# Graph attention with edge features on one core: how the eight heads' scores of each edge are made leaky and summed

## The chip, the cores and the metric

The kernel runs on one core of a Trainium2 chip. The metric is the device time of one execution in microseconds (us), taken as the median of several runs. The profile that is read here is one further execution under the hardware profiler. The engines are TensorE (PE for its products, PEld for its weight loads, which overlap them), VectorE (DVE), ScalarE (ACT), GpSimd (POOL) and SyncE (SP, which issues most DMAs).

## The reference

One graph attention layer over 12,500 nodes and 412,500 edges (each node has an edge to itself), with 128 features a node, 64 an edge, and 8 heads. The attention weight of an edge comes from a small network with two leaky rectifiers; the softmax runs over all edges of the graph at once.

```python
h = node_features @ Wn + bn
q = node_features @ Wq + bq
k = node_features @ Wk + bk
v = node_features @ Wv + bv
eh = edge_features @ We + be
src, tgt = (edge_index[0], edge_index[1])
attn_in = jnp.concatenate([q[src], k[tgt], eh], axis=-1)
hmid = jax.nn.leaky_relu(attn_in @ A1 + b1, SLOPE)
scores = jax.nn.leaky_relu(hmid @ A2 + b2, SLOPE)
w = jax.nn.softmax(scores.mean(axis=-1), axis=0)
out = jax.ops.segment_sum(w[:, None] * v[tgt], src, num_segments=num_nodes)
y = h + out
...
return gamma * (y - mu) / jnp.sqrt(var + EPS) + beta
```

The change touches the line of `scores` and the mean over the heads behind it.

## The kernel before

Edges arrive sorted by their target. The kernel cuts them into four chunks (`CHUNKS`). A first stage goes through a chunk's edges in tiles of 128: TensorE makes for every edge a row of 257 numbers (the place of its source in a block, 128 hidden values, 128 values of `v`), ScalarE copies it out of PSUM (line 652), and GpSimd scatters 128 rows at a time into a table in HBM (line 603), ordered by blocks of source nodes.

A second stage then works through the table. There are 98 blocks of source nodes, and each chunk has its part of every block, so 392 blocks in all (`blocks`), numbered through the chunks. A block of chunk 0, 1, 2 or 3 holds `ct` = 8, 11, 11 or 7 tiles of 128 edges, and its tiles are taken in `nq` = 2, 3, 3 or 2 groups of four (`QUAD`).

The second stage of chunk c runs beside the first stage of chunk c + 1; that of chunk 3 runs alone at the end. `interleave` mixes the jobs step by step when the program is built, and the engines' queues keep the order in which it was written (`manual_schedule`). Inside the second stage a plan by hand sets the order: `at(when, turn_, job, i)` puts a job of block i into a step, and jobs of one step are ordered by `turn_`. [...]

The steps of a block that matter here, in their order:

- `turn` (line 719, TensorE): four transposes (723) and three products (726) put the hidden values of four tiles into `h_ps`.
- `steep` (729): ScalarE makes `low`, 0.2 times these (734), VectorE takes the maximum and writes it back into `rows_of` (735).
- `heads_of` (738, TensorE, 743): product with `A2`. The result `s_ps` is one PSUM bank of 128 x 512; group q of four tiles has rows 32q to 32q + 31, of which the first 8 are the heads, and the columns are 4 x 128 edges.
- `add_bias` (747, ScalarE, 750): adds `b2` and copies `s_ps` to `z` in SBUF.
- `leaky` (752, VectorE, 754): z = max(0.2 z, z) over 32nq x 512.
- `by_slot` (756, TensorE, 760): for each of the four columns of tiles a product of `z` with `heads`, a matrix of zeros and ones, which sums the eight heads and turns edges onto partitions. Each fp32 product of this kind has two records of a weight load and two of a product in the profile, eight pairs a block.
- `scores` (764, VectorE, 768 to 774): a mask for empty slots, the older maximum, the sum of the two, and the largest of each partition, `top`.
- `turn_top` (777, TensorE), `top_of_all` (781, VectorE), `spread_top` (784, TensorE), `exponentials` (790 and 793 on VectorE, 795 on ScalarE): the largest score of the whole block, and the exponentials.
- `weights` (809, VectorE) and `products` (818, TensorE): the weighted sum of the values for an older block; `add_sums` (823, VectorE) adds it to `acc`.

In the steps of the next block, `steep` of its first group stands just ahead of `by_slot` in the plan, and on VectorE line 735 of that group stands just ahead of `scores`. Behind `scores` VectorE has line 823 or `weights`, then line 781. The turn of the next group follows `turn_top` on TensorE.

Of the kernel before, what the change touches and what calls it, by code (L numbers as in the profile page):

```python
# [13 lines left out]
ALU = mybir.AluOpType  # L14
AX = mybir.AxisListType
# [4 lines left out]
P = 128  # L20
D = 128
DE = 64
H = 8
EPS = 1e-5
SLOPE = 0.2
# [5 lines left out]
QUAD = 4  # L31
# [67 lines left out]
def kernel(ctx: ExitStack, tc: tile.TileContext, n_edges, x, src, dst, ea, w_nv, w_qt, w_kt,  # L99
# [12 lines left out]
    nc = tc.nc  # L112
# [10 lines left out]
    for i, share in enumerate(CHUNKS):  # L123
        n = NG - g0 if i == len(CHUNKS) - 1 else max(1, round(NG * share))
# [7 lines left out]
    blocks = []  # L132
# [40 lines left out]
    ident = const.tile([P, P], FP, name="ident")  # L173
# [3 lines left out]
    ones = const.tile([P, P], FP, name="ones")  # L177
# [47 lines left out]
    heads = const.tile([P, 4], FP, name="heads")  # L225
# [336 lines left out]
    most_of = late.tile([P, NTN], FP, name="most_of")  # L562
# [116 lines left out]
    def second_stage():  # L679


        rows_of, qws, plss, state = {}, {}, {}, {}
# [66 lines left out]
            state["z"] = p3.tile([P, 512], FP, name="z")  # L749
            nc.scalar.activation(state["z"][:n, :], state["s_ps"][:n, :], AF.Identity, bias=b2_col[:n, :])  # L750

        def leaky(i):
            z = state["z"][:32 * blocks[i][3], :]
            nc.vector.scalar_tensor_tensor(z, z, SLOPE, z, op0=ALU.mult, op1=ALU.max)  # L754

        def by_slot(i):

            nq = blocks[i][3]
            for j in range(QUAD):
                nc.tensor.matmul(state["s_ps"][:, 0:nq * QUAD].rearrange("p (q j) -> p j q", j=QUAD)[:, j, :],  # L760
                                 lhsT=state["z"][:32 * nq, ts(j, P)], rhs=heads[:32 * nq, 0:nq], start=True, stop=True,
                                 skip_group_check=True)

        def scores(i):

            _, b, ct, _, _ = blocks[i]
            none = ps.tile([P, most_tiles], FP, name="none")[:, 0:ct]
            nc.vector.tensor_scalar(none, rows_of[i][:, 0:ct, 0:1].rearrange("p j r -> p (j r)"), 0.0, -1e30,
                                    op0=ALU.is_equal, op1=ALU.mult)
            state["score", i] = score = ps.tile([P, most_tiles + 1], FP, name="score")  # L770
            nc.vector.tensor_copy(score[:, ct:ct + 1], most_of[:, b:b + 1])
            nc.vector.tensor_add(score[:, 0:ct], state["s_ps"][:, 0:ct], none)
            state["top"] = ps.tile([P, 1], FP, name="top_of")
            nc.vector.tensor_reduce(state["top"], score[:, 0:ct], AX.X, ALU.max)

        def turn_top(i):
            nc.tensor.transpose(state["s_ps"][0:1, P:2 * P], state["top"], ident)

        def top_of_all(i):
            state["top1"] = ps.tile([1, 1], FP, name="top1_of")  # L780
            nc.vector.tensor_reduce(state["top1"], state["s_ps"][0:1, P:2 * P], AX.X, ALU.max)

        def spread_top(i):
            nc.tensor.matmul(state["s_ps"][:, 2 * P:2 * P + 1], lhsT=ones[0:1, :], rhs=state["top1"], start=True, stop=True,
                             skip_group_check=True)

        def exponentials(i):
            _, b, ct, _, _ = blocks[i]
            before = (b - 1) % NTN
            nc.vector.tensor_max(most_of[:, b:b + 1], state["s_ps"][:, 2 * P:2 * P + 1], most_of[:, before:before + 1])  # L790

            shift = ps.tile([P, 1], FP, name="shift_of")
            nc.vector.tensor_scalar(shift, most_of[:, b:b + 1], -1.0 / H, None, op0=ALU.mult)
            score = state["score", i][:, 0:ct + 1]
            nc.scalar.activation(score, score, AF.Exp, bias=shift, scale=1.0 / H)
# [32 lines left out]
        def at(when, turn_, job, *args):  # L828
            plan_of.setdefault(when, []).append((turn_, len(plan_of[when]) if when in plan_of else 0, job, args))

        for i, (c, b, ct, nq, i0) in enumerate(blocks):
            t = 2 * i0
            at(load_at(i), 2, load, i)
            at(t - 7, 3, places, i)
            at(t - 6, 0, put_places, i)
            at(t - 5, 0, spread_places, i)
            at(t - 1, 3, select, i)
            for q in range(nq):
                at(t + 2 * q, 1, turn, i, q)
                at(t + 2 * q + 1, 0, steep, i, q)  # L840
            t += 2 * nq
            at(t - 1, 3, heads_of, i)
            at(t, 0, add_bias, i)
            at(t, 3, leaky, i)
            at(t + 1, 0, by_slot, i)
            at(t + 1, 3, scores, i)
            at(t + 2, 0, turn_top, i)
            at(t + 2, 3, top_of_all, i)
            at(t + 3, 0, spread_top, i)
            at(t + 3, 2, exponentials, i)  # L850
            at(t + 4, 3, add_weights, i)
            t = 2 * i0 + LAG
            for q in range(nq):
                at(t + 2 * q - 1, 0, weights, i, q)
                at(t + 2 * q, 1, products, i, q)
            at(t + 2 * nq - 1, 0, add_sums, i)
# [5 lines left out]
    def load_at(i):  # L862

        _, _, _, nq, i0 = blocks[i]
        t = 2 * i0 - (17 if nq > 2 else 11)
        if i >= BUFS:
            _, _, _, nq, i0 = blocks[i - BUFS]
            t = max(t, 2 * (i0 + nq - 1) + LAG)
        return t
# [11 lines left out]
    def other_edges():  # L881

        with tc.tile_pool(name="others", bufs=1) as op, tc.tile_pool(name="others_ps", bufs=1, space=PSUM) as ops_:
# [5 lines left out]
            with tc.For_i(0, turns, 1) as g:  # L889
# [63 lines left out]
                with tc.For_i(0, NTN, 1) as b:  # L953
# [8 lines left out]
                    nc.vector.tensor_add(a, a, bank[:, 0:D])  # L962

    second = second_stage()
    ends = [load_at(c * NTN) for c in range(NC)]
    ends.append(2 * (blocks[-1][4] + blocks[-1][3]) + LAG)
    for c in range(NC + 1):
# [4 lines left out]
        if c > 0:  # L972
            n = ends[c] - ends[c - 1]
# [16 lines left out]
    with tc.tile_pool(name="last", bufs=3) as lp:  # L990
        for t0 in range(0, NTN, NGRP):
            n = min(NGRP, NTN - t0)
# [52 lines left out]
```

## Time and profile before

| | |
|---|---|
| runs | 6621.57 us median of 3 (6614.75 to 6624.29) |
| profiled execution | 6612.85 us, span 6611.2 us |
| mean granted TensorE clock | 0.893 |
| TensorE products, weight loads | busy 5118.9 us (77%), 3487.2 us (53%) |
| VectorE, ScalarE, GpSimd | busy 4308.9 us (65%), 2132.6 us (32%), 3319.2 us (50%) |
| line 754, `leaky`, VectorE | 392 times, 0.683 us median |
| line 760, `by_slot`, TensorE | 3136 loads, 3136 products, busy 392.1 and 412.4 us |
| line 723, transposes of `turn` | 3626 loads, 3626 products, busy 438.7 and 577.1 us |

How to read it: a busy time is the time in which the engine has at least one instruction under way. A wait is written as "engine tile line <- engine tile line: us in total, times, longest": the left one's engine stood idle until the right one was done. "issue" is an idle time for which the profile shows no wait. In a timeline line come start and length in us, engine, source line, operation, what is written and read, its shape, and in brackets the idle time before it with what ended it. The page's slices cut the span into 40 equal parts of 165 us and give busy tenths.

### The profile page before, as it was taken

To read this page: it belongs to the slowest core of one execution; us is meant where nothing else is said; L and a number is where in the kernel's file an instruction comes from. 1 tells how busy PE (TensorE), PEld (TensorE's weight loads), DVE (VectorE), ACT (ScalarE), POOL (GpSimd) and SP (SyncE) were. 2 spreads that over 40 slices of the span, in tenths; PEclk is the share of its full clock that TensorE was granted. 3 is DMA by queue.
4 is the path that set the end of the run, shared out by engine and by line. 5 is a ranking of instruction groups with operands and counts; after the bars stand their busy time and mean duration, and the time that the engine had idled before them with its cause. 6 is when DMAs were issued, how large, how long until landed. Compare 5 with 4: busy or idle time off the path is not lost. (4 is left out here: it accounts for less than half of the span.)

```text
span 6611.2 us, 98770 instructions
## 1 busy us (share of the span) xinstructions
PE 5118.9 (77%) x32071; PEld 3487.2 (53%) x32430; DVE 4308.9 (65%) x13992; ACT 2132.6 (32%) x4818; POOL 3319.2 (50%) x3334
## 2 busy tenths in 40 slices
PE   0466376665289999997599999998999999988881
PEld 0222143333166666665366676666667676655550
DVE  0889454434177777775377777776666666777778
ACT  0123122222134434343134444443334333333331
POOL 3000177777457777776267777775555555200000
PEclk9866568778689999998699999999999999999995
DMA  9222655445878888888979889887888888655543
GB/s 176 83 85 85 199 171 159 158 152 157 248 231 270 262 266 264 264 264 249 265 261 298 287 292 290 286 294 257 276 275 276 275 282 274 215 167 168 167 155 117
DMA packets 598421, 1474.37 MB, mean 223 GB/s; under 512 B 117236, under 2 KB 245586, under 8 KB 559880
## 3 DMA queue, kind: packets, MB, share of 16 engines
q1 hardware_dynamic: 405972, 963.63, 48.7%
q0 software_dynamic: 162544, 450.05, 19.9%
q10 hardware_dynamic: 29380, 54.29, 2.3%
q8 instruction: 256, 4.19, 0.3%
q14 instruction: 269, 2.20, 0.1%
HBM read 893.55 MB, written 574.02 MB: 222 GB/s over the span
## 5 line engine op out<-in xcount | busy, mean ns | idle before, releaser
L603 POOL DMA_INDIRECT tab<-row,slots x3223 | 3264.4, 1013 | 2271.8 <-issue 718.0
L666 PE MATMUL row_ps<-w_ea,ea_t 128*128 128x256 f32 x3224 | 1100.4, 426 | 382.0 <-ACT row L652 343.9
L652 ACT ACTIVATE row<-row_ps 128x512 f32<-128x512 f32 x1612 | 933.4, 589 | 589.0 <-PE row_ps L669 567.5
L818 PE MATMUL o_ps<-rows_of,w 128*128 128x128 f32 x7252 | 1079.6, 291 | 7.9 <-DVE w L809 7.0
L809 DVE TENSOR_SCALAR w<-iota_f,rows_of,score 128x128 f32<-128x128 f32 x3626 | 1021.6, 353 | 5.8
L735 DVE TENSOR_TENSOR rows_of<-h_ps,low 128x512 f32<-128x512 f32 (+1 forms) x980 | 634.7, 648 | 530.3 <-ACT low L734 515.0
L666 PEld LDWEIGHTS row_ps<-w_ea,ea_t 128*128 128x128 f32 x3224 | 599.2, 209 | 648.9 <-ACT row L652 467.8
L818 PEld LDWEIGHTS o_ps<-rows_of,w 128*128 128x128 f32 x7252 | 914.2, 195 | 35.9 <-DVE w L809 17.6
L734 ACT ACTIVATE low<-h_ps 128x512 f32<-128x512 f32 (+1 forms) x980 | 552.7, 564 | 929.2 <-PE h_ps L726 909.2
L726 PE MATMUL h_ps<-pls,qw 128*128 128x512 bf16 (+1 forms) x2581 | 740.0, 367 | 115.0 <-DVE pls L715 93.6
L492 DVE TENSOR_REDUCE num<-run 128x5 f32<-128x500 f32 x646 | 433.3, 671 | 467.9 <-PE run L455 466.9
L669 PE MATMUL row_ps<-kv,offs 126*128 126x256 bf16 x3224 | 670.6, 291 | 8.9 <-DVE offs L641 5.1
L723 PE MATMUL h_ps<-ident,rows_of 128*128 128x128 f32 x3626 | 577.1, 279 | 0.0
L743 PE MATMUL s_ps<-rows_of,a_sb 128*32 128x512 f32 (+1 forms) x1960 | 454.6, 580 | 71.7 <-DVE most_of L790 39.4
L723 PEld LDWEIGHTS h_ps<-ident,rows_of 128*128 128x128 f32 x3626 | 438.7, 144 | 109.3 <-issue 81.6
L669 PEld LDWEIGHTS <-offs 126*128 126x128 bf16 x3224 | 339.4, 105 | 291.6 <-issue 64.7
L760 PEld LDWEIGHTS s_ps<-heads,z 96*128 96x128 f32 (+1 forms) x3136 | 392.1, 194 | 185.2 <-DVE z L754 162.1
L648 ACT ACTIVATE row<-place 128x4 f32<-128x4 bf16 x806 | 163.3, 203 | 974.8 <-DMA tab<-row,slots 940.4
L760 PE MATMUL s_ps<-heads,z 96*128 96x3 f32 (+1 forms) x3136 | 412.4, 252 | 70.8 <-DVE z L754 69.7
L448 DVE TENSOR_TENSOR one<-bins_b,block 128x500 bf16<-128x500 bf16 x646 | 431.7, 668 | 33.8 <-PE run L455 24.0
L750 ACT ACTIVATE z<-s_ps,b_col 64x512 f32<-64x512 f32 (+1 forms) x392 | 267.2, 682 | 532.0 <-PE s_ps L743 531.5
L726 PEld LDWEIGHTS <-qw 128*128 128x128 bf16 x2940 | 291.7, 99 | 218.8 <-issue 109.6
(172 smaller groups left out, 4930.9 us busy)
## 6 DMA issues: line engine op xcount, KB each, us to landing
rows_of<-tab SPq DMA_DIRECT2D x196, 1413.5 KB
ea_t<-in_ea SPq DMA_DIRECT2D x200, 512.0 KB
offs<-off_d SPq DMA_DIRECT2D x403, 252.0 KB
rows_of<-tab SPq DMA_DIRECT2D x98, 1028.0 KB
rows_of<-tab SPq DMA_DIRECT2D x98, 899.5 KB
tab<-blank SPq DMA_DIRECT2D x294, 257.0 KB
pls<-pl_d SPq DMA_DIRECT2D x196, 352.0 KB
tab<-row,slots POOLq DMA_INDIRECT x3223
```

Of the source, the lines that this page charges most:

```text
L603: i = nc.gpsimd.indirect_dma_start(out=tabs[c][:, :], out_offset=bass.IndirectOffsetOnAxis(ap=slots[c][:m, t:t + 1], axis=0), in_=row[:m, ...
L652: nc.scalar.activation(row[:, :, at, 1:ROW], bank, AF.Copy)
L666: nc.tensor.matmul(bank[:, :, 0:D], lhsT=ea_g[:, ts(k, P)], rhs=w_ea, start=True, stop=False, skip_group_check=True)
L669: nc.tensor.matmul(bank[:, b, :], lhsT=sel[:, ts(b * halves + k, P)], rhs=kv, start=False, stop=True, skip_group_check=True)
L723: nc.tensor.matmul(h_ps[:, ts(j, P)], lhsT=rows_of[i][:, q * QUAD + j, 1:D + 1], rhs=ident, is_transpose=True, start=j == 0, stop=False, s ...
L726: nc.tensor.matmul(h_ps[:, 0:m * P], lhsT=qws[i][:, ts(k, D)], rhs=plss[i][:, q * QUAD * P:(q * QUAD + m) * P], start=False, stop=k == 2, ...
L734: nc.scalar.activation(low, h_ps, AF.Copy, scale=SLOPE)
L735: nc.vector.tensor_max(rows_of[i][:, q * QUAD:q * QUAD + m, 1:D + 1], h_ps.rearrange("p (j e) -> p j e", j=m), low.rearrange("p (j e) -> p ...
L743: nc.tensor.matmul(state["s_ps"][32 * q:32 * (q + 1), 0:m * P], lhsT=a2_sb, rhs=rows_of[i][:, q * QUAD:q * QUAD + m, 1:D + 1], start=True, ...
L760: nc.tensor.matmul(state["s_ps"][:, 0:nq * QUAD].rearrange("p (q j) -> p j q", j=QUAD)[:, j, :], lhsT=state["z"][:32 * nq, ts(j, P)], rhs= ...
L809: nc.vector.tensor_scalar(w, iota_f, rows_of[i][:, t, 0:1], state["score", i][:, t:t + 1], op0=ALU.is_equal, op1=ALU.mult)
L818: nc.tensor.matmul(state["o_ps"][:, 0:D], lhsT=w, rhs=rows_of[i][:, t, D + 1:ROW], start=t == 0, stop=t == ct - 1)
```

## The change

`leaky` goes, and `by_slot` transposes instead of multiplying: for each of the four columns of tiles, `z` (32nq x 128) is turned into `s_ps` as 128 edges x 32nq rows. `scores` then reads of these only the eight used rows of each group, with edges on partitions, and makes three VectorE instructions of them: 0.2 times the scores, the maximum of that and the scores, and the sum over the heads. Their results lie in `z`, which is free by then. The sum `by` takes the place of `s_ps` in the old addition. `turn_top`, `top_of_all`, `spread_top` and `exponentials` use other columns of `s_ps`. `heads` is still built, and no longer used.

```diff
@@ -749,45 +749,45 @@
             state["z"] = p3.tile([P, 512], FP, name="z")
             nc.scalar.activation(state["z"][:n, :], state["s_ps"][:n, :], AF.Identity, bias=b2_col[:n, :])
 
-        def leaky(i):
-            z = state["z"][:32 * blocks[i][3], :]
-            nc.vector.scalar_tensor_tensor(z, z, SLOPE, z, op0=ALU.mult, op1=ALU.max)
-
         def by_slot(i):
 
-            nq = blocks[i][3]
+            n = 32 * blocks[i][3]
             for j in range(QUAD):
-                nc.tensor.matmul(state["s_ps"][:, 0:nq * QUAD].rearrange("p (q j) -> p j q", j=QUAD)[:, j, :],
-                                 lhsT=state["z"][:32 * nq, ts(j, P)], rhs=heads[:32 * nq, 0:nq], start=True, stop=True,
-                                 skip_group_check=True)
+                nc.tensor.transpose(state["s_ps"][:, j * n:(j + 1) * n], state["z"][:n, ts(j, P)], ident[:n, :n])
 
         def scores(i):
 
-            _, b, ct, _, _ = blocks[i]
+            _, b, ct, nq, _ = blocks[i]
+            z = state["s_ps"][:, 0:QUAD * nq * 32].rearrange("p (j q h) -> p q j h", j=QUAD, q=nq)[:, :, :, 0:H]
+            steep = state["z"][:, 0:nq * QUAD * H].rearrange("p (q j h) -> p q j h", q=nq, j=QUAD)
+            nc.vector.tensor_scalar(steep, z, SLOPE, None, op0=ALU.mult)
+            nc.vector.tensor_max(steep, steep, z)
+            by = state["z"][:, 3 * P:3 * P + nq * QUAD]
+            nc.vector.tensor_reduce(by.rearrange("p (q j) -> p q j", j=QUAD), steep, AX.X, ALU.add)
             none = ps.tile([P, most_tiles], FP, name="none")[:, 0:ct]
             nc.vector.tensor_scalar(none, rows_of[i][:, 0:ct, 0:1].rearrange("p j r -> p (j r)"), 0.0, -1e30,
                                     op0=ALU.is_equal, op1=ALU.mult)
             state["score", i] = score = ps.tile([P, most_tiles + 1], FP, name="score")
             nc.vector.tensor_copy(score[:, ct:ct + 1], most_of[:, b:b + 1])
-            nc.vector.tensor_add(score[:, 0:ct], state["s_ps"][:, 0:ct], none)
+            nc.vector.tensor_add(score[:, 0:ct], by[:, 0:ct], none)
             state["top"] = ps.tile([P, 1], FP, name="top_of")
             nc.vector.tensor_reduce(state["top"], score[:, 0:ct], AX.X, ALU.max)
 
         def turn_top(i):
-            nc.tensor.transpose(state["s_ps"][0:1, P:2 * P], state["top"], ident)
+            nc.tensor.transpose(state["s_ps"][0:1, 3 * P:4 * P], state["top"], ident)
 
         def top_of_all(i):
             state["top1"] = ps.tile([1, 1], FP, name="top1_of")
-            nc.vector.tensor_reduce(state["top1"], state["s_ps"][0:1, P:2 * P], AX.X, ALU.max)
+            nc.vector.tensor_reduce(state["top1"], state["s_ps"][0:1, 3 * P:4 * P], AX.X, ALU.max)
 
         def spread_top(i):
-            nc.tensor.matmul(state["s_ps"][:, 2 * P:2 * P + 1], lhsT=ones[0:1, :], rhs=state["top1"], start=True, stop=True,
+            nc.tensor.matmul(state["s_ps"][:, 0:1], lhsT=ones[0:1, :], rhs=state["top1"], start=True, stop=True,
                              skip_group_check=True)
 
         def exponentials(i):
             _, b, ct, _, _ = blocks[i]
             before = (b - 1) % NTN
-            nc.vector.tensor_max(most_of[:, b:b + 1], state["s_ps"][:, 2 * P:2 * P + 1], most_of[:, before:before + 1])
+            nc.vector.tensor_max(most_of[:, b:b + 1], state["s_ps"][:, 0:1], most_of[:, before:before + 1])
 
             shift = ps.tile([P, 1], FP, name="shift_of")
             nc.vector.tensor_scalar(shift, most_of[:, b:b + 1], -1.0 / H, None, op0=ALU.mult)
@@ -841,7 +841,6 @@
             t += 2 * nq
             at(t - 1, 3, heads_of, i)
             at(t, 0, add_bias, i)
-            at(t, 3, leaky, i)
             at(t + 1, 0, by_slot, i)
             at(t + 1, 3, scores, i)
             at(t + 2, 0, turn_top, i)
```

## The prediction

> **What bounds the kernel now.** I read the page's slices first, to find stages with different limits, then the starts of lines 603 and 754 to cut the span into them, then the waits in each stage, and the timeline where one engine pattern repeats without change.
>
> ```profile
> PE   0466376665289999997599999998999999988881
> ...
> DVE  0889454434177777775377777776666666777778
> ...
> POOL 3000177777457777776267777775555555200000
> ```
>
> Line 754, the instruction that the change removes, runs 392 times, once a block, from 1840 to 6455 us. Its blocks fall into four stages of 98: A, 1840 to 3170, beside chunk 1's scatters; B, 3200 to 4600, beside chunk 2's; C, 4610 to 5717, beside chunk 3's; D, 5725 to 6455, with nothing beside it (the POOL row ends in zeros). From first to last start of line 754, a block takes 13.6, 14.4, 11.4 and 7.53 us. Waits of stage A, then of stage C (us in total, times, longest):
>
> ```profile
> ACT row L648 <- DMA tab<-row,slots: 292.0, 141, 6.9
> POOL tab L603 <- issue: 206.1, 676, 0.4
> ...
> POOL tab L603 <- ACT row L652: 62.0, 77, 14.8
> ```
>
> ```profile
> POOL tab L603 <- ACT row L652: 365.0, 177, 7.2
> ...
> DVE pls L715 <- DMA pls<-pl_d: 98.8, 61, 4.6
> ```
>
> In A the scatters set the pace: 952 of them in 1330 us, each 0.97 us and a gap of 0.30 us (952 x 1.27 = 1209), and ScalarE waits for their landings. In C GpSimd waits for rows instead, and TensorE (988 us busy of 1050) with a DMA round trip for `pls` sets it; B lies between. Stage D is one block repeated; this is the timeline of one, start and length in us, idle before it in brackets:
>
> ```profile
> 6107.48 0.42 PEld L723 LDWEIGHTS h_ps<-ident,rows_of 128*128 128x128 f32 x4 [0.84 <-issue]
> ...
> 6107.98 0.81 PE L726 MATMUL h_ps<-pls,qw 128*128 128x512 bf16 x2
> 6108.32 0.68 DVE L754 SCALAR_TENSOR_TENSOR z<-z 64x512 f32<-64x512 f32 x1 [1.00 <-ACT z L750]
> ...
> 6108.89 0.60 ACT L734 ACTIVATE low<-h_ps 128x512 f32<-128x512 f32 x1 [0.60 <-PE h_ps L726]
> 6109.06 0.96 PEld L760 LDWEIGHTS s_ps<-heads,z 64*128 64x128 f32 x8 [0.77 <-DVE z L754]
> 6109.06 1.05 PE L760 MATMUL s_ps<-heads,z 64*128 64x2 f32 x8 [0.27 <-DVE z L754]
> 6109.52 0.69 DVE L735 TENSOR_TENSOR rows_of<-h_ps,low 128x512 f32<-128x512 f32 x1 [0.51 <-ACT low L734]
> 6110.04 0.74 PEld L818 LDWEIGHTS o_ps<-rows_of,w 128*128 128x128 f32 x6
> ...
> 6110.59 0.16 DVE L774 TENSOR_REDUCE top_of<-score 128x1 f32<-128x7 f32 x1
> ...
> 6110.81 0.08 PEld L777 LDWEIGHTS s_ps<-ident,top_of 128*1 128x1 f32 x1
> ...
> 6111.02 0.35 DVE L823 SCALAR_TENSOR_TENSOR acc<-acc,score,o_ps 128x128 f32<-128x128 f32 x1 [0.27 <-PE o_ps L818]
> ...
> 6111.28 1.11 DVE L809 TENSOR_SCALAR w<-iota_f,rows_of,score 128x128 f32<-128x128 f32 x4
> ...
> 6112.31 0.27 DVE L781 TENSOR_REDUCE top_of<-s_ps 1x1 f32<-1x128 f32 x1
> ...
> 6112.63 0.29 PEld L784 LDWEIGHTS s_ps<-top_of,ones 1*128 1x128 f32 x2 [1.01 <-DVE top_of L781]
> ...
> 6114.02 0.14 PEld L743 LDWEIGHTS s_ps<-rows_of,a_sb 128*32 128x32 f32 x4
> ```
>
> The reader should see two things. Line 754 sits in an idle hole of VectorE (1.00 before it, 0.51 after it, where line 735 waits for ScalarE's `low`). From line 735 to 781 VectorE then has no rest but 0.27 before line 823, and TensorE waits for the end of that row at line 784 (1.01). The next block starts at 6115.01.
>
> [...] eight loads of line 760 take 0.96, a step of 0.11, at 64 rows as at 96. [...] here 5 elements cost 0.15 us (line 496) and 500 cost 0.67 (line 492). [...] 128 elements from PSUM cost 0.27 (line 781). [...]
>
> **Part by part.**
> TensorE, removed: eight load and product pairs a block (392 blocks), steps of 0.11: after the first load of line 760 the next line's load comes 0.89 to 0.98 later. Added: four transposes. Line 723 shows four: the next line's load comes 0.39 to 0.43 later. The moving side shrinks to 64 or 96 columns, but the load is still 128 columns, so I take no more off. Saving 0.45 us a block; at most 0.6, and nothing if the transposes ran in two passes as the products do (line 723's count is one for each tile, against that).
>
> Removed wait: line 760 waited for line 754. It would now wait for ScalarE's line 750, done at 6108.29, before TensorE is through with line 726. TensorE's own idle time there is 0.12, 0.07, 0.24 and 0.29 us a block in A, B, C and D (from the gaps of the first product).
>
> VectorE, removed: one instruction of 0.683 us. Added in `scores`, between line 735 and the old body: a product by 0.2, a maximum, a sum, on 64 elements (A, D) or 96 (B, C). By the two rows above, 0.15 + elements x 1.04 ns: 0.22 or 0.25 each; dependent neighbours stand 0.03 apart (lines 772 and 774: 0.20 for 0.17). So 0.74 or 0.84; the first can begin under the tail of line 735, as line 768 did by 0.07: about 0.7 and 0.8. No row has such strided PSUM reads; bounds 0.18 and 0.30 each, 0.55 to 0.95 together. VectorE's sum is nearly unchanged, but the work moves from the hole to the full row. The three moved score addresses (`turn_top`, `top_of_all`, `spread_top`) move no instruction: nothing. No DMA, no SP or POOL instruction changes.
>
> Stage D, counted from 6107.48. Before: `low` ends 2.01, line 735 runs 2.04 to 2.73, line 774 ends 3.27, line 777 starts 3.33, line 823 3.54, line 809 3.80, line 781 4.83 to 5.10, line 784 5.15, line 743 6.54, next block 7.53. After: TensorE is free at 1.3 and has transposed by 1.75, with `products` (0.74) and the places done by 2.55, 0.8 earlier. That buys nothing, since `low` and line 735 hang on line 726, whose time hasn't changed. Line 774 ends at 3.27 + 0.7 = 3.97; line 777 waits for it until 4.03. Line 823 now has its `o_ps` long before, so its 0.27 of idling is eaten: 0.7 - 0.25 = 0.45 late. The four weights and line 781 are behind it in the queue, so line 784 starts at 5.60, and eight products, line 743 and the next block follow: 7.98. TensorE's second `turn` (line 777 plus about 1.0) is done at 5.1, before 5.60. So +0.45 a block, x 97 = +44 us; 0.30 to 0.70 by the bounds: +29 to +68.
>
> Stages A to C. Here other work stands between, so I compared for each block the start of line 777 with both new limits: TensorE's path earlier by 0.45 plus its idle time at line 760, and line 774's new end (plus 0.7 or 0.8, less what VectorE gains where line 754 held it up and no idle hole follows). The mean move of line 777 is -0.38 in A, -0.24 in B, -0.13 in C. In C a block with a long wait at line 760 gains 0.4 to 0.9, one without it loses 0.45. Times 98: -37, -24, -12. Not all of it counts. In A GpSimd waits for rows only 62 us, so I take a fifth: -8. In B half: -12. In C, where nothing else is the bound, -10. Line 781 comes later behind the longer queue in some blocks: +4.
>
> Sum: 44 - 8 - 12 - 10 + 4 = +18. The profiled execution took 6612.85 (span 6611.2 and 1.65 around it): 6631. The median of the runs, 6621.57, lies 8.7 above it, and I set the forecast by it: **6640 us**.
>
> **Rivals.**
> *Faster.* In B and C TensorE keeps its whole saving, since VectorE, rid of line 754 early, catches up in later holes: (0.52 + 0.69) x 98 = -119, with A's -8 and D's +44: -83, 6539; half of it -23, 6598. For it: TensorE is over 90% busy in B and C, and line 777 has a median slack of 0.88 in B. Against: 0.32 in C, less than the 0.8 put in. It decides once A to C give back more than 44, that is 0.15 us a block.
> *No change.* Gains of 35 to 50 there against 44 in D: 6617 to 6633.
> *Slower still.* A to C gain nothing, since scatter landings and the `pls` round trip set them, and the VectorE instructions cost their upper bound: +68, 6690.
> *Not what it says.* The transposes take eight steps: D is +44 all the same, as TensorE waits for line 774 there, and A to C lose their gains: +48, 6670.
>
> **How the numbers follow.** A measurement of this kernel can tell about 0.2%, 13 us, from no change. Chances: slower by 13 to 45 us 0.36 (likeliest; its own range 6635 to 6667), slower still or not what it says 0.12, no change 0.20, faster 0.32. The range 6565 to 6676 leaves out the faster rival's far half and the far end of slower still.
>
> **What would show it.** Right: line 777 in D waits for line 774 about 0.75 us on every block, line 760's place shows no VectorE wait, D's block goes from 7.53 to about 8.0, VectorE's busy time stays within 40 us, and A keeps its length. Wrong: D's block at or under 7.6 (then the VectorE price or order was misread), or B and C shorter by over 50 us together.

## The result: 1.04% slower, and the loss sits in the last stage

| | before | changed |
|---|---|---|
| median of 6 runs each | 6619.09 us (6608.32 to 6625.54) | 6687.62 us (6668.9 to 6696.66) |
| profiled execution | 6612.85 us | 6696.04 us, span 6694.3 us |
| TensorE products, loads busy | 5118.9, 3487.2 us | 4980.2, 3258.2 us |
| VectorE busy | 4308.9 us | 4281.6 us |
| mean granted TensorE clock | 0.893 | 0.883 |

The ratio is 1.0104, with a 95% interval of 1.0092 to 1.0117. The forecast was +18 us on the median; it is +68.5. The two profiled executions lie 83 us apart.

The stages, cut as in the prediction but by the first and last start of line 750, which both kernels have, give lengths in us:

| stage | before | changed | difference |
|---|---|---|---|
| A, chunk 0 | 1313.6 | 1308.3 | -5.3 |
| B, chunk 1 | 1408.2 | 1408.1 | -0.1 |
| C, chunk 2 | 1110.3 | 1091.1 | -19.2 |
| D, chunk 3 | 730.8 | 827.3 | +96.5 |

What remains, 11 us, lies ahead of the first block and between the stages. The sum of A to C, -25, meets the forecast's -26; the parts don't, since B was to gain 12 us and stood still. A single pair of profiles can't show so little: two profiles with the same code in these stages, on one chip, differ by 10 us there (the kernel before and the new way in chunk 3 alone, below). D was to lose 44 us and lost 96.5: 8.53 us a block and not 7.98.

The slices of the changed kernel's page, TensorE and its clock:

```profile
PE   0466376666288888886689999988898888888881
...
PEclk9866567788689999998799999999999999988885
```

In the last slices before the end (the final one belongs to the normalisation) the clock's digit is 8, where stages B and C have mostly 9. The windows view has the granted clock as a number; after the five engines' busy times come PEclk, DMA share and GB/s. Stage D before, then stage D of the changed kernel:

```profile
5725.00:6455.00 730.00, 639.97 (x4119) 437.11 (x4166) 542.18 (x2037) 225.92 (x483) 0.00 (x0) 1.00 0.50 163
```

```profile
5712.00:6538.00 826.00, 667.91 (x3731) 407.02 (x3778) 519.87 (x2230) 225.66 (x482) 0.00 (x0) 0.90 0.44 144
```

TensorE runs fewer instructions and is busy for longer, at a clock of 0.90 where it had 1.00. The timeline of one block of stage D in the changed kernel, to be laid beside the block in the prediction (count from the first line):

```profile
6109.36 0.42 PEld L723 LDWEIGHTS h_ps<-ident,rows_of 128*128 128x128 f32 x4 [0.84 <-issue]
...
6110.59 0.32 PEld L756 LDWEIGHTS s_ps<-ident,z 64*128 64x128 f32 x4 [0.42 <-ACT z L750]
...
6110.98 0.74 PEld L818 LDWEIGHTS o_ps<-rows_of,w 128*128 128x128 f32 x6
...
6111.39 0.69 DVE L735 TENSOR_TENSOR rows_of<-h_ps,low 128x512 f32<-128x512 f32 x1 [1.96 <-ACT low L734]
...
6112.00 0.21 DVE L763 TENSOR_SCALAR z<-s_ps 128x64 f32<-128x64 f32 x1
...
6112.25 0.22 DVE L764 TENSOR_TENSOR z<-z,s_ps 128x64 f32<-128x64 f32 x1
...
6112.50 0.22 DVE L766 TENSOR_REDUCE z<-z 128x8 f32<-128x64 f32 x1
6112.64 0.16 DVE L768 TENSOR_SCALAR none<-rows_of 128x7 f32<-128x7 f32 x1
...
6113.04 0.16 DVE L774 TENSOR_REDUCE top_of<-score 128x1 f32<-128x7 f32 x1
6113.11 0.34 DVE L823 SCALAR_TENSOR_TENSOR acc<-acc,score,o_ps 128x128 f32<-128x128 f32 x1
6113.25 0.08 PEld L777 LDWEIGHTS s_ps<-ident,top_of 128*1 128x1 f32 x1 [1.51 <-DVE top_of L774]
6113.25 0.27 PE L777 MATMUL s_ps<-ident,top_of 128*1 128x128 f32 x1 [1.22 <-DVE top_of L774]
...
6114.72 0.29 PEld L784 LDWEIGHTS s_ps<-top_of,ones 1*128 1x128 f32 x2 [0.77 <-DVE top_of L781]
```

The order of events is the forecast one. TensorE is done with its transposes and products early, then stands for 1.22 us at line 777 until VectorE has the three new instructions and the old ones behind it through. Line 784 starts 5.36 after the block's begin (5.15 before): the queue alone costs 0.21. The block that ended at 6109.36 had begun at 6101.62, 7.74 earlier. But the next one is not like it (same kernel, the timeline further on):

```profile
6115.02 1.78 PEld L818 LDWEIGHTS o_ps<-rows_of,w 128*128 128x128 f32 x8
...
6117.03 1.73 PE L743 MATMUL s_ps<-rows_of,a_sb 128*32 128x512 f32 x4
...
6118.69 0.42 PEld L723 LDWEIGHTS h_ps<-ident,rows_of 128*128 128x128 f32 x4 [1.47 <-issue]
```

The same eight loads take 1.78 us where they took 0.97, and the four products 1.73 where they took 1.05. The windows view of these microseconds and of the ones after them:

```profile
6114.90:6118.40 3.50, 3.50 (x14) 2.08 (x13) 2.19 (x9) 0.30 (x1) 0.00 (x0) 0.52 0.38 131
6118.40:6132.00 13.60, 10.34 (x67) 6.39 (x66) 8.57 (x38) 4.38 (x9) 0.00 (x0) 1.00 0.52 152
```

For about 3.4 us TensorE ran at half its clock. In the clock records of stage D this comes every 17.07 us (46 of 47 distances): one window of 3.41 us at 0.5, four at 1.0. Of 97 block distances in stage D 48 are long, 9.34 us on average, and the others 7.73; a pair, 17.07, is as long as five windows. Before, stage D has no halved window in this profile (a second one, on another chip, has one, near the end of the stage). By this reading 0.21 of the 1.00 us a block is the queue and 0.79 the clock; the experiments below test it.

### The profile page after: what moved, and what is told of

The parts are those of the page before. It is cut to its first block, busy times and chain, and to the rows that moved or that the text cites. A ratio compares the mean times of both kernels' runs of the same rounds, so it can differ in the third digit from the quotient of the medians.

```text
span 6694.3 us, 96026 instructions
## 1 busy us (share of the span) xinstructions
PE 4980.2 (74%) x30503; PEld 3258.2 (49%) x30862; DVE 4281.6 (64%) x14776; ACT 2126.6 (32%) x4818; POOL 3288.4 (49%) x3334
## 5 line engine op out<-in xcount | busy, mean ns | idle before, releaser
L818 PE MATMUL o_ps<-rows_of,w 128*128 128x128 f32 x7252 | 1104.8, 296 | 15.7 <-DVE w L809 15.4
L818 PEld LDWEIGHTS o_ps<-rows_of,w 128*128 128x128 f32 x7252 | 946.9, 201 | 52.0 <-DVE w L809 24.4
L743 PE MATMUL s_ps<-rows_of,a_sb 128*32 128x512 f32 (+1 forms) x1960 | 493.3, 623 | 94.2 <-DVE most_of L790 58.2
L641 DVE TENSOR_SCALAR offs<-offs,third 126x1024 bf16<-126x1024 bf16 x403 | 198.6, 493 | 316.3 <-DMA offs<-off_d 316.1
L715 DVE TENSOR_SCALAR pls<-pls,part 128x1408 bf16<-128x1408 bf16 (+2 forms) x392 | 213.1, 544 | 279.5 <-DMA pls<-pl_d 279.0
```

What stands on the lines that cost most here:

```text
L743: nc.tensor.matmul(state["s_ps"][32 * q:32 * (q + 1), 0:m * P], lhsT=a2_sb, rhs=rows_of[i][:, q * QUAD:q * QUAD + m, 1:D + 1], start=True, ...
L818: nc.tensor.matmul(state["o_ps"][:, 0:D], lhsT=w, rhs=rows_of[i][:, t, D + 1:ROW], start=t == 0, stop=t == ct - 1)
```

## Theories

*Clock.* The longer VectorE row makes TensorE wait (1.22 us at line 777), and the transposes leave it less to do; in some windows it then works too little, the clock is halved in the next one (48 halved windows in stage D), and that costs 0.79 us a block (97 blocks, 77 us).

*Queue.* VectorE's order makes the whole loss; the clock record goes with the waits and costs nothing of its own.

## Experiments

The runs in one group share one chip, and chips differ: on four of them the kernel before took 6619, 7225, 7284 and 6562 us. Where it took 7225, stages A and B of the kernel with the transposes three times are longer by 250 and 280 us than those of the changed kernel on the first chip. So each run is held against the kernel before on its own chip, and absolute times in the expectations, which were written from the first chip, are read as differences. Stage D hardly depends on the chip (7.53 and 7.54 us a block). All kernels here keep the rest of the code.

| run | us | before, same chip | ratio, 95% interval | D, us a block | clock in D |
|---|---|---|---|---|---|
| transposes three times | 7247.88 | 7225.27 | 1.0029 (1.0017 to 1.0041) | 7.74 | 1.00 |
| new way in chunks 0 to 2 | 7222.88 | 7225.27 | 0.9995 (0.9982 to 1.0008) | 7.53 | 1.00 |
| leaky kept | 7157.76 | 7225.27 | 0.9913 (0.9885 to 0.9940) | 7.25 | 1.00 |
| weights early | 7217.04 | 7225.27 | 0.9988 (0.9979 to 0.9998) | 7.31 | 1.00 |
| changed, again | 7377.92 | 7284.37 | 1.0121 (1.0095 to 1.0147) | 8.37 | 0.92 |
| transposes twice | 7305.04 | 7284.37 | 1.0027 (1.0014 to 1.0039) | 7.74 | 1.00 |
| three times, again | 7302.24 | 7284.37 | 1.0023 (1.0011 to 1.0036) | 7.74 | 1.00 |
| leaky kept, weights early | 7207.48 | 7284.37 | 0.9894 (0.9868 to 0.9920) | 7.20 | 1.00 |
| leaky kept, again | 6523.38 | 6562.11 | 0.9941 (0.9920 to 0.9961) | 7.23 | 1.00 |
| new way in chunk 3 alone | 6640.92 | 6562.11 | 1.0124 (1.0095 to 1.0153) | 8.37 | 0.92 |

### More work for TensorE

```diff
-            for j in range(QUAD):
+            for j in list(range(QUAD)) * (3 if blocks[i][0] == NC - 1 else 1):
                 nc.tensor.transpose(state["s_ps"][:, j * n:(j + 1) * n], state["z"][:n, ts(j, P)], ident[:n, :n])
```

> The changed kernel, with the transposes of a block of the last chunk issued three times over (the same result into the same place), 0.86 us more TensorE work a block, in a stretch where TensorE waits 1.2 us anyway. Clock theory: of the last stage's 1.00 us a block more, 0.21 is the longer VectorE queue and 0.79 the halved TensorE clock, which comes because TensorE has too little to do; with more to do the clock stays at 1.00, a block takes 7.7 to 7.8 us, and the whole 6605 to 6625 us, about 75 us less than the changed kernel. Queue theory: the waits for VectorE make the loss, the clock only goes with them; more TensorE work leaves the block at 8.5 or lengthens it, 6685 us or more.

Beside the kernel before it loses 0.29%, or 22.6 us, which is stage D's 0.21 x 97 = 20 us. The block of 7.74 us is the one that the clock theory expected. The whole time misses what it expected, 14 us less to 6 us more than the kernel before. The changed kernel had not run on that chip, so another chip had both, and a kernel with the transposes twice:

> The changed kernel itself, beside the two that only repeat its transposes in the last chunk, so that all three are read on one chip. Clock theory: the last stage again at 8.5 us a block with the TensorE clock at 0.5 for one window of 3.41 us in five, about 75 us over the kernel with three transposes. If the halved clock was an accident of one run: 7.7 us a block, and the same time as the kernel with three.

> The transposes of a block of the last chunk issued twice over: 0.43 us more TensorE work a block, as much as the change took away. Clock theory [...]: either 7.74 us a block at clock 1.00 [...], or a few drops, between 7.74 and 8.5. Queue theory: 8.5, as for one.

> The transposes three times over, beside the changed kernel on one chip. Clock theory: 7.74 us a block in the last stage at clock 1.00, and the whole 70 to 85 us less than the changed kernel. Queue theory: no less than the changed kernel.

Stage D in the windows view, first the changed kernel, then with transposes twice, then three times:

```profile
6412.00:7222.00 810.00, 652.03 (x3731) 392.72 (x3778) 519.98 (x2231) 225.43 (x482) 0.00 (x0) 0.92 0.44 146
```

```profile
6406.00:7155.00 749.00, 615.04 (x4118) 391.24 (x4166) 519.73 (x2229) 225.64 (x482) 0.00 (x0) 1.00 0.48 159
```

```profile
6391.00:7140.00 749.00, 639.39 (x4507) 415.31 (x4554) 519.88 (x2230) 225.40 (x482) 0.00 (x0) 1.00 0.48 158
```

With 388 or 776 more transposes stage D is 61 us shorter in the windows, at an unchanged VectorE time (520 us) and in an unchanged VectorE order. The whole is 73 us (twice) and 76 us (three times) less than the changed kernel. TensorE's busy time even falls with twice, from 652 to 615, since nothing of it runs at half clock. The queue theory has no place for that; the clock theory's numbers, 7.74 us and 70 to 85 us, are met. That the whole differs by more than stage D is within the spread of the changed kernel's own runs (7363.65 to 7384.93).

### Where the change pays and where it costs

One kernel takes the new way in chunks 0 to 2 (stages A to C), one in chunk 3 alone. Both keep `leaky`, the products with `heads` and the addition of `s_ps` for the other blocks:

```diff
+        def turned(i):
+            return blocks[i][0] < NC - 1
...
+            if not turned(i):
+                at(t, 3, leaky, i)
```

> The new way in chunks 0 to 2, the old one in chunk 3 (the last stage). Both theories: the last stage is as before, 7.53 us a block at clock 1.00. Stages A to C keep what the changed kernel has there, about 5, 0 and 19 us less than before: 6590 to 6610 us. If A to C's gain were paid for by the last stage (work moved, not saved), it would be 6620 or more.

> The new way in chunk 3 alone, the old one in chunks 0 to 2. If the whole loss sits in the last stage: 8.3 to 8.5 us a block there with the clock halved at times, 75 to 100 us more than before in all, as much as the changed kernel. If half or more comes from A to C: under 60 us more.

The new way in A to C alone moves the kernel by -2.4 us, between -13 and +6 by the interval: no gain that can be seen, where the first pair of profiles had shown -25. It lies between the two cases named (9 to 29 us less, or no gain), and the interval reaches into both. In chunk 3 alone it costs 78.8 us, within the 75 to 100 expected and as much as the whole change (68.5 and 93.6 us on two other chips). So the loss is stage D's, and A to C give next to nothing back.

### VectorE's row without the two extra instructions

```diff
+            at(t, 3, leaky, i)
...
-            steep = state["z"][:, 0:nq * QUAD * H].rearrange("p (q j h) -> p q j h", q=nq, j=QUAD)
-            nc.vector.tensor_scalar(steep, z, SLOPE, None, op0=ALU.mult)
-            nc.vector.tensor_max(steep, steep, z)
...
-            nc.vector.tensor_reduce(by.rearrange("p (q j) -> p q j", j=QUAD), steep, AX.X, ALU.add)
+            nc.vector.tensor_reduce(by.rearrange("p (q j) -> p q j", j=QUAD), z, AX.X, ALU.add)
```

> The old VectorE leaky instruction on z in its idle hole, then the four transposes, then one sum over the heads on VectorE in place of three instructions: TensorE has as little work as in the changed kernel, VectorE's full row is only 0.1 to 0.2 us longer than before. Queue theory: the last stage returns to 7.5 to 7.6 us a block at clock 1.00, whole 6585 to 6605 us. Clock theory: TensorE still has 0.45 us less to do in the same period than before, so the clock halves at times in the last stage and a block takes 8.0 us or more: 6630 us or more.

7.25 us a block at clock 1.00, 67 us less than the kernel before. Both expectations miss, in opposite directions. The clock theory as I had put it there looked at TensorE's work a block, and that doesn't decide: it is as little as in the changed kernel, and the clock holds. But the blocks are shorter, so TensorE's products are busy for 86% of stage D (602.98 of 703 us), against 80% in the changed kernel (652.03 of 810) and 82% with the transposes twice (615.04 of 749); whether it is the mean share that decides is taken up below. And the queue theory missed that the block becomes shorter than before. The timeline of a second run of this kernel (its line 778 is the old 777, and 824 the old 823):

```profile
6105.03 0.42 PEld L723 LDWEIGHTS h_ps<-ident,rows_of 128*128 128x128 f32 x4 [0.84 <-issue]
...
6105.87 0.68 DVE L754 SCALAR_TENSOR_TENSOR z<-z 64x512 f32<-64x512 f32 x1 [0.78 <-ACT z L750]
...
6107.06 0.69 DVE L735 TENSOR_TENSOR rows_of<-h_ps,low 128x512 f32<-128x512 f32 x1 [0.51 <-ACT low L734]
...
6107.67 0.21 DVE L767 TENSOR_REDUCE z<-s_ps 128x8 f32<-128x64 f32 x1
...
6108.27 0.34 DVE L824 SCALAR_TENSOR_TENSOR acc<-acc,score,o_ps 128x128 f32<-128x128 f32 x1
...
6108.41 0.08 PEld L778 LDWEIGHTS s_ps<-ident,top_of 128*1 128x1 f32 x1 [0.66 <-DVE top_of L775]
```

The old leaky instruction is back in its hole, ahead of line 735, which it doesn't delay. The row behind line 735 has one new instruction and not three. Line 824 starts 3.24 after the block's begin, where its twin had 3.54 before and 3.75 in the changed kernel: it no longer waits for `o_ps`, since TensorE's transposes are quicker than the products were (0.46 us for the four, 1.05 for the eight). That is the 0.3 us a block. The second run had a profile of the kernel before beside it, on the same chip:

> The kernel before with a profile of its own, on the chip of its two companions, so that stages can be compared on one chip: the last stage 7.53 us a block at clock 1.00; stages A to C give the base.

> The kernel with the leaky instruction kept, beside a profile of the kernel before. If TensorE's saving is real and was given back at line 777 in the changed kernel, A to C are 30 to 50 us shorter than before, most of it where TensorE is the bound (B and C), and the last stage 27 us: 60 to 75 us in all. If the first comparison was chance, A to C differ by under 15 us.

The kernel before took 6555.18 us in that profile. Stage D went from 731.7 to 701.4 us, -30; A, B and C went by +7, -0.4 and -1.5. The whole is 38.7 us less by the medians, not 60 to 75. So stage D's gain is repeated, but the 30 to 50 us in A to C are a miss: the 40 us that the first comparison left for them (67 - 27) didn't come again on this chip. Whether they belong to the chips whose stages A and B are longer stays open.

### VectorE's order

```diff
-                at(t + 2 * q - 1, 0, weights, i, q)
+                at(t + 2 * q - 2, 0, weights, i, q)
```

> The changed kernel with the weights (line 809's) made one step earlier, so that in the last stage four of them fall into the idle hole before line 735 and the largest score no longer queues behind them. If VectorE's order sets the last stage's loop, line 781 comes about 1 us earlier, TensorE waits less at line 784, and the last stage takes 7.0 to 7.4 us a block, with the clock at 1.00 since the period is shorter: 6540 to 6600 us. If the clock still falls, 7.6 to 8.2 us and 6600 to 6660. If the order of VectorE doesn't matter, 8.5 and 6685.

In chunks 1 and 2 this kernel makes the weights of a block's first group from scores whose exponentials have not been taken yet, with the same instructions; so it doesn't compute the layer, and serves for its times alone. Stage D is 7.31 us a block, within the 7.0 to 7.4 of the first case: line 781 no longer waits behind four weights. So the queue's 0.21 can be bought back too. The whole is 8 us less than the kernel before, where the first case had 19 to 79. Stages A and B are longer than in the kernel with the new way in chunks 0 to 2 (1579.9 and 1706.8 against 1563.7 and 1680.2 us, same chip), so the move was made in chunk 3 alone. There it was joined with the leaky instruction in its hole:

```diff
-                at(t + 2 * q - 1, 0, weights, i, q)
+                at(t + 2 * q - (2 if c == NC - 1 else 1), 0, weights, i, q)
```

> The old leaky instruction in its hole, four transposes and one sum, and in the last chunk the weights one step earlier, where line 795's exponentials are already taken. VectorE's order: line 781 no longer stands behind four weights, so the last stage falls from 7.25 to 6.8 to 7.0 us a block, 25 to 45 us off the kernel with the leaky instruction kept, if the clock holds at 1.00; if TensorE's work within a window is then too small, the clock halves at times and the gain is lost, 7.3 us or more.

7.20 us a block, against the 6.8 to 7.0 expected: a miss. The four weights now stand between the leaky instruction and line 735 (this kernel's 810 is the old 809):

```profile
6607.46 0.60 ACT L734 ACTIVATE low<-h_ps 128x512 f32<-128x512 f32 x1 [0.60 <-PE h_ps L726]
6607.50 1.10 DVE L810 TENSOR_SCALAR w<-iota_f,rows_of,score 128x128 f32<-128x128 f32 x4
...
6608.52 0.68 DVE L735 TENSOR_TENSOR rows_of<-h_ps,low 128x512 f32<-128x512 f32 x1
```

`low` is there at 6608.06, and line 735 starts at 6608.52: the hole is too small for both. Its whole time, 1.06% under the kernel before, can't be told from that of the leaky instruction alone (0.59% and 0.87%; the intervals overlap with the second). Either kernel is faster than the kernel before, and the joined one, on its chip, than the changed kernel (7207.48 against 7377.92 us).

### What the clock goes by

For all runs I laid windows of 3.413 us, the step of the grid on which the edges of the clock records lie (last section), on these edges and added up in each the time in which TensorE had a product or a load under way. In stage D of the changed kernel the 48 full-clock windows ahead of a halved one hold 51 to 57%, and the 146 full-clock windows with no halved one behind them 63% or more. In its second run it is 49 to 57%, but nine windows of 54 to 58% had no halving behind them. With the transposes twice no window of 219 falls under 58%, and none is halved; with them three times, in the kernel with leaky kept and in the joined one all stay at 64% or more. Three halvings in stage D don't fit, each in its last 20 us or so: one behind a window of 69% in the kernel with leaky kept, one behind 65% in the kernel with early weights, and one behind 77% in the second profile of the kernel before. What made them stays open.

TensorE's mean work over a stage doesn't decide. In stage C of the kernel before its products are busy for 94% of the time, and 17 windows there are halved; in stage D they are busy for 88%, and none is (639.97 of 730 us, the line in the section on the result). Stage C:

```profile
4610.00:5660.00 1050.00, 988.09 (x6519) 735.63 (x6610) 708.90 (x2454) 410.19 (x966) 556.70 (x554) 0.97 0.84 275
```

What goes with a halving is little work in the window just ahead of it, but not with a sharp edge. In stages A to C of the first two profiles a halved window came behind 56 of the 61 full-clock windows under 45%, behind 14 of the 54 from 45 to 58%, and behind 9 of the 1933 above. So a window under 45% is nearly always followed by a halved one, one above 58% hardly ever, and in between something decides that this sum of busy time doesn't show. The reading comes from the traces; no run varied the work of one window alone.

## Why the prediction was wrong

**The side was right, the size was not.** Slower was the likeliest case, by 18 us. The measured 68.5 us more put the median at 6687.62 us, beyond the range's end of 6676.

**The step that failed** is the term of stage D, "So +0.45 a block, x 97 = +44 us". The stage lost 96.5 us. The term had two errors, of opposite signs. The chain of waits behind it was right, but sized too high: line 774's start moved from 3.11 to 3.68, by 0.57 and not 0.7. Line 768 begins 0.08 before the third new instruction ends, and line 772 now follows 771 by 0.13 and not 0.19. And line 823 had 0.36 us to give and not 0.25 (it began 0.43 after line 774's start, and now 0.07). 0.57 - 0.36 = 0.21 a block, or 20 us. What the sum lacked was the clock. Every duration came from a stage with the clock at 1.00, and I let TensorE be idle for longer and kept its durations. The changed block has 1.22 us at line 777 and 0.38 at line 784 in which TensorE does nothing, and with them the clock was halved at times: +0.79 a block. The kernels with more transposes show it, since they fill a part of these waits, leave VectorE's row as it is, and have blocks of 7.74 us at a clock of 1.00.

That the sum would have been right without the clock is luck. With the transposes twice and three times, where nothing in stage D is halved, the kernel is 18 to 23 us slower than before, and 18 was forecast; but D's 44 was 20, and the 26 from A to C were next to nothing.

**A to C.** The forecast, -26 with line 781's share, stands against -25 in the first pair of profiles and -2.4 in the whole time of the kernel that has the new way there alone. TensorE does save: its products' busy time falls by 139 us over the span although stage D's halved clock adds to it. In the changed kernel a good part of that comes back as waits at line 777, as the comparison block by block had it. TensorE's waits in A to C there:

```profile
PEld s_ps L777 <- DVE top_of L774: 163.1, 182, 2.8
...
PE s_ps L777 <- DVE top_of L774: 112.7, 141, 2.3
```

Before, the load of line 777 waited 8.1 us there for VectorE in all. The old wait of products at line 760, 39.8 us, is gone; 112.7 us at line 777 have come.

But that these waits are why A to C gain nothing is not shown. In the second run of the kernel with leaky kept, the products of line 778 (the old 777) wait only 22.3 us for VectorE in A to C, and TensorE's products are busy for 126 us less than in the kernel before on the same chip (3361 against 3487, from 1820 to 5630 us). Yet these stages are 5 us longer there, and C, where the forecast had nothing else as the bound, is 1.5 us shorter. What else sets their length stays open.

**Prices.** The transposes cost what line 723 said: the next line's load comes 0.39 after their first, against 0.98 before. The new VectorE instructions took 0.21 to 0.22 us on 64 elements, as worked out (0.22). Two readings behind the prices were a little low, without effect: line 496 takes 0.15 us at the least, 0.16 in the median, and the scatters of stage A 1.02 us on average (969.31 us for 952), 0.97 being their median. VectorE's busy time changed by -27 us, within the 40 named.

**Rivals.** The faster one needed 44 us from A to C; they gave 25 at most. "Slower still" came nearest in time (6690), but by another mechanism: neither the scatter landings nor dearer VectorE instructions made it. The transposes did what they say.

**What was to show it.** Line 777 waits on every block of stage D, 1.22 us in the median and not 0.75, because TensorE also arrives earlier. The block of 8.0 us doesn't occur in this profile: there are blocks of about 7.73 and of about 9.34.

## What to carry to other kernels

Before an instruction is moved to a busier engine, look where its place in that engine's queue is: 0.68 us of VectorE time in a hole was free, and 0.65 us behind the last thing that arrives was not. When a change takes work from TensorE or makes it wait, look at the granted clock of the same stage in both traces before any duration is compared. This kernel lost more by a freed TensorE than by a loaded one: with its transposes issued twice or three times it was over 70 us faster. Repeating an instruction in a wait is a quick test for that.

## What the hardware showed

The halved clock needs no long pause. In stage D of the changed kernel's first profile the two longest gaps between products are 1.34 and 1.33 us, every other is 1.23 us or less, and still 48 windows are halved. The clock records of that profile hold two values, 0.5 and 1.0. Their edges all lie on one grid of 3.41333 us, to within 0.01 us over the whole span; so the windows don't begin anew with a block, and a pair of blocks, one of 9.34 and one of 7.73 us, is as long as five of them, 17.07 us. In stage D 46 of the 47 distances between halved windows are five windows, and one is three.

The pattern isn't kept everywhere: stage D of the changed kernel took 8.53 us a block in the first profile and 8.37 in its second, where 39 of 97 distances were long and not 48. In that one, and in the kernel with the new way in chunk 3 alone, the distance between halved windows is 34 times five windows and four times fourteen.
